# TensorE's order within a step of a graph network's edge loop: transposes, products and sums apart, a bank of the second layer behind each, relus by group

## The chip, the cores and the metric

The kernel runs on one core of a Trainium2 chip. The metric is the device time of one execution in microseconds (us). Each engine of the core (TensorE for matmuls, VectorE, ScalarE, GpSimd, SyncE) works through its own list of instructions in order and waits on semaphores that the others raise. In the profile PE is TensorE's matmuls, PEld its weight loads, DVE VectorE, ACT ScalarE, POOL GpSimd and SP SyncE. A matmul on fp32 data is two weight loads and two matmuls in the trace; a transpose, or a matmul on bf16 data, is one of each.

## What is computed

One layer of a graph network over 6,250 nodes with 128 features and 100,000 edges that are sorted by their destination, then a residual and a layer norm:

```python
msg_in = jnp.concatenate([node_features[row], node_features[col]], axis=-1)
h = jax.nn.relu(msg_in @ Wm1 + bm1)          # 256 -> 256
h = jax.nn.relu(h @ Wm2 + bm2)               # 256 -> 256
messages = h @ Wm3 + bm3                     # 256 -> 128
agg = jax.ops.segment_sum(messages, col, num_segments=num_nodes)
count = jax.ops.segment_sum(jnp.ones(...), col, num_segments=num_nodes)
agg = agg / jnp.clip(count, 1.0)[:, None]
node_in = jnp.concatenate([node_features, agg], axis=-1)
upd = jax.nn.relu(node_in @ Wn1 + bn1) @ Wn2 + bn2
return layernorm(x + node_features + upd)
```

`row` is the source of an edge and `col` its destination.

## The kernel before

The first layer is split by its input: x times the upper half of Wm1 (atab) and x times the lower half (btab, in bf16 terms) are made once for all nodes and stored in DRAM. Then 98 steps (NP) go over the edges, each with two groups of 512 edges, four tiles of 128. Wm3 is applied to the sums of a node's edges, not to each edge.

What a step p does, as its iteration of the main loop (from line 978 on) issues it:

- `fetch` (L598): for the next step, eight indirect gathers of atab rows by source on POOL (L607) and a few plain loads of btab rows on SP (L620) into one of two row buffers. Some gathers wait for a mark on TensorE's work, so that they keep its pace: `MARKS` (L588) ties gather 0 to the sums, gather 4 to the 13th matmul of a second layer, gather 6 to the first product. The loads wait for the last product that reads the buffer (`last_product`).
- `make_hot` (VectorE, L640 and L642): one-hot matrices from the destinations, to spread btab rows over edges and to sum edges into a window of nodes.
- `turned(p - 3)` (TensorE, L770): six transposes of an earlier step's sums; VectorE adds the result to the accumulator (L743, later in the loop L779).
- `node_steps(p, 0)`, and later `node_steps(p, 1)`: parts of the node network for nodes that have all their edges (TensorE L811, L817, L844), planned for certain steps.
- `first_layer(p)` (L660): for both groups 32 transposes of gathered rows (L666, 64 rows of the array each), then for both groups the products of btab rows with the one-hot matrix added on top (L674 eight of 256 columns, from step 59 on L683 sixteen of 128). All of it goes to the four banks of `ph`. Then two relus on ScalarE (L692), each over both groups, 128x1024, into h1.
- `summed(p - 2)` (L734, from step 82 on L724): eight matmuls with a one-hot matrix as weights, in columns of 32; ScalarE copies the bank out as `part` (L752).
- `second_layer` for each group of step p - 1 (L706): two banks for a group, each four matmuls (L711), and behind each bank VectorE takes the larger of it and the negative bias (L714) into `h2s`.

TensorE does all this in exactly the order written, since no scheduler moves instructions. The working banks are four tiles, used in turn by the sums, the second layer, `turned` and the node parts; whoever takes one waits until its last reader is done.

Of the kernel before, what the change touches and what calls it, by code (L numbers as in the profile page):

```python
# [13 lines left out]
AF = mybir.ActivationFunctionType  # L14
ALU = mybir.AluOpType
# [5 lines left out]
P = 128  # L21
# [9 lines left out]
def kernel(  # L31
# [511 lines left out]
    with edge, tc.tile_pool(name="wk", bufs=2) as wk, tc.tile_pool(  # L543
# [116 lines left out]
        def first_layer(got, ohts, nts, step):  # L660
            for i, ((ag, _, _), nt) in enumerate(zip(got, nts)):
                for c in range(HC):
                    for j in range(GT):
                        for h in range(nt // 2):
                            half = slice(h * HP, (h + 1) * HP)
                            nc.tensor.matmul(ph[:, i, h, c, j * HP:(j + 1) * HP], ag[half, j, c * P:(c + 1) * P],  # L666
                                             ident[half, half], is_transpose=True, start=(c == 0 and j == 0),
                                             stop=False, skip_group_check=True)
            for i, ((_, bw, paired), nt) in enumerate(zip(got, nts)):
                for c in range(HC):  # L670
                    if paired:
                        for h in range(2):
                            half = slice(h * HP, (h + 1) * HP)
                            matmul = nc.tensor.matmul(ph[:, i, h, c, :], bw[half, 0, c * P:(c + 1) * P],  # L674
                                                      ohts[half, i, :], start=False, stop=True,
                                                      skip_group_check=True)
                            pace(step + 1, "products", (i * HC + c) * 2 + h, matmul)
                            last_product[step] = matmul
                        continue
                    for k in range(2):  # L680
                        for h in range(nt // 2):
                            half = slice(h * HP, (h + 1) * HP)
                            matmul = nc.tensor.matmul(ph[:, i, h, c, k * P:(k + 1) * P],  # L683
                                                      bw[half, k, c * P:(c + 1) * P],
                                                      ohts[half, i, k * P:(k + 1) * P], start=False, stop=True,
                                                      skip_group_check=True)
                            if k == 0:
                                pace(step + 1, "products", (i * HC + c) * 2 + h, matmul)
                            last_product[step] = matmul
            h1 = next_h1()  # L690
            if nts == [GT, GT]:
                made = [nc.scalar.activation(h1[:, :, c, :].rearrange("p i (h e) -> p i h e", h=2),  # L692
                                             ph[:, :, :, c, :], AF.Relu, bias=b1[:, c:c + 1]) for c in range(HC)]
                for one in made:
                    follows(("h1", step % 2), one)
                for one in made:
                    keep(("h1", step % 2), one)
                return h1
            for i in reversed(range(len(nts))):
                nh = nts[i] // 2  # L700
                for c in range(HC):
                    nc.scalar.activation(h1[:, i, c, :nh * 2 * P].rearrange("p (h e) -> p h e", h=nh),
                                         ph[:, i, :nh, c, :], AF.Relu, bias=b1[:, c:c + 1])
            return h1

        def second_layer(h1, h2, nt, step, before):  # L706
            for j0 in range(0, nt, 2):
                ph2 = bank()
                for j in range(j0, j0 + 2):
                    for c in range(HC):  # L710
                        matmul = nc.tensor.matmul(ph2[:, j - j0, :], h1[:, c, j * P:(j + 1) * P],  # L711
                                                  w2[:, c, :], start=(c == 0), stop=(c == HC - 1))
                        pace(step + 2, "second", before + j * HC + c, matmul)
                made = nc.vector.tensor_tensor(h2[:, j0:j0 + 2, :H], ph2, nb2.to_broadcast([P, 2, H]), op=ALU.max)  # L714
                follows("copied", made)
                keep("largest", made)
# [261 lines left out]
        for i in range(NP + 7):  # L978
# [42 lines left out]
            if p == 0:  # L1021
                whole(x_part(X_FIRST, bank, (nc.scalar, nc.vector)))
# [100 lines left out]
```

## Time and profile before

| | us |
|---|---|
| median of 3 runs | 1339.16 (1331.02 to 1341.98) |
| the profiled execution | 1348.45 |
| its span | 1346.7 |
| TensorE's matmuls busy | 1237.1 |
| its weight loads busy | 935.8 |
| GpSimd busy | 793.6 |
| VectorE busy | 618.8 |
| ScalarE busy | 335.5 |

The tables take the first 85 us or so, the steps most of the rest. Matmuls overlap in the array, so the duration of one is longer than the distance to the next; distances are read from the start times of the timeline. A row of the timeline merges instructions of one kind: its start and how long it lasts in us, the engine, the line and the operation, how many, and in brackets how long the engine had been idle before it, with what ended that. A row of a window gives its length, and for each engine the busy us and the number of instructions.

### The profile page before, as it was taken

The numbers are of one execution on the slowest core, as the hardware profiler recorded it, in microseconds if no ns is written. First come the engines' busy times: TensorE is split into PE (matmuls) and PEld (weight loads), VectorE is DVE, ScalarE is ACT, GpSimd is POOL, SyncE is SP. The second block draws the span as 40 slices with busy tenths as digits, with TensorE's granted clock in tenths as the row PEclk, the third lists the DMA queues.
The fourth block names the chain that finished last, engine by engine and source line by source line (L and its number), as shares of the span: only waits on it lengthen the run. The fifth ranks groups of instructions, "written<-read, shape, count | busy, mean of one in ns | idle before, by whom it ended". The sixth has DMA issues, their size and how long they took to land.

```text
span 1346.7 us, 26320 instructions
## 1 busy us (share of the span) xinstructions
PE 1237.1 (92%) x10288; PEld 935.8 (69%) x10289; DVE 618.8 (46%) x1502; ACT 335.5 (25%) x500; POOL 793.6 (59%) x854
## 2 busy tenths in 40 slices
PE   8988998999999999999999998989988999999996
PEld 6746666776776667766766766767767677777784
DVE  6754333333333334443444443534445454555675
ACT  4741221122122112222221222221222212223232
POOL 6666665665666666666666665655655655556531
PEclk9999999999999999999999999999999899999998
DMA  7963443433433334334343444434444434344320
GB/s 224 336 207 105 124 116 99 114 106 101 112 108 112 101 107 115 106 108 129 108 110 113 123 114 118 134 111 125 131 115 120 123 111 137 107 118 122 108 58 24
DMA packets 113876, 163.66 MB, mean 122 GB/s; under 512 B 24730, under 2 KB 74592, under 8 KB 113728
## 3 DMA queue, kind: packets, MB, share of 16 engines
q0 software_dynamic: 38160, 103.75, 27.5%
q1 hardware_dynamic: 67292, 44.97, 10.8%
q10 hardware_dynamic: 8292, 13.18, 3.4%
q8 instruction: 82, 1.34, 0.4%
q14 instruction: 50, 0.41, 0.1%
HBM read 142.35 MB, written 19.86 MB: 120 GB/s over the span
## 4 chain that ended last, share of the span: by engine, by line
PE 89%; issue 6%; DVE 4%; DMA 0%; ACT 0%; POOL 0%; DVEq 0%; SPq 0%; ACTq 0%; POOLq 0%
PE bank L711 53%; PE bank L734 11%; PE ph L666 9%; PE bank L770 3%; PE ph L674 2%; PE pbt L315 2%; PE ph L683 2%; PE bank L844 2%; PE bank L811 1%; PE bank L817 1%; PE bank L724 1%; PE pxu L426 1%; DVE h L714 1%; DVE acc L779 0%; DVE span_i L267 0%
## 5 line engine op out<-in xcount | busy, mean ns | idle before, releaser
L607 POOL DMA_INDIRECT rows<-atab,srcT x784 | 746.1, 952 | 485.2 <-issue 166.8
L711 PE MATMUL bank<-w,h 128*128 128x256 f32 x3128 | 722.6, 386 | 8.0 <-DVE h L714 4.1
L711 PEld LDWEIGHTS bank<-w,h 128*128 128x128 f32 x3128 | 592.5, 192 | 139.3 <-issue 52.5
L714 DVE TENSOR_TENSOR h<-bank,nb 128x512 f32<-128x512 f32 x391 | 264.9, 690 | 600.8 <-PE bank L711 407.4
L692 ACT ACTIVATE h<-ph,b 128x1024 f32<-128x1024 f32 x194 | 205.6, 1110 | 789.2 <-remote 393.5
L666 PE MATMUL ph<-ident,rows 64*128 64x64 f32 x3128 | 134.6, 226 | 38.1 <-issue 36.6
L734 PE MATMUL bank<-h,oh 128*32 128x257 f32 x1312 | 155.5, 409 | 12.4 <-issue 1.3
L666 PEld LDWEIGHTS ph<-ident,rows 64*128 64x128 f32 x3128 | 117.2, 141 | 49.7 <-issue 46.5
L734 PEld LDWEIGHTS bank<-h,oh 128*32 128x32 f32 x1312 | 46.8, 112 | 93.8 <-issue 77.1
L743 DVE TENSOR_TENSOR acc<-acc,bank 128x96 f32 x328 | 83.5, 255 | 40.2 <-remote 18.4
L770 PEld LDWEIGHTS bank<-ident,part 64*128 64x128 f32 x681 | 31.1, 137 | 48.1 <-issue 27.6
L770 PE MATMUL bank<-ident,part 64*128 64x64 f32 x681 | 46.8, 237 | 12.6 <-DVE h L714 8.6
L315 PE MATMUL pbt<-w,xT 128*128 128x256 f32 x196 | 47.6, 388 | 5.9 <-DVE rest L340 3.0
L752 ACT COPY part<-bank 128x257 f32<-128x257 f32 x114 | 42.1, 375 | 24.4 <-PE bank L711 17.3
L315 PEld LDWEIGHTS pbt<-w,xT 128*128 128x128 f32 x196 | 36.5, 194 | 13.4 <-DVE rest L340 4.2
L674 PE MATMUL ph<-oht,rows 64*128 64x256 bf16 x472 | 40.1, 275 | 4.2 <-issue 4.2
L683 PE MATMUL ph<-oht,rows 64*128 64x128 bf16 x620 | 32.7, 225 | 10.7 <-issue 10.0
L642 DVE TENSOR_TENSOR oh<-iota_w,dloc 128x256 f32<-128x256 f32 x82 | 34.3, 418 | 0.0
L779 DVE TENSOR_TENSOR acc<-acc,bank 128x63 f32 x126 | 27.8, 221 | 13.3 <-remote 4.5
L683 PEld LDWEIGHTS <-rows 64*128 64x128 bf16 x620 | 23.2, 99 | 14.8 <-issue 14.7
L640 DVE TENSOR_SCALAR oht<-db,iota_p 128x512 bf16<-128x512 bf16 x98 | 31.8, 324 | 0.0
L674 PEld LDWEIGHTS <-rows 64*128 64x128 bf16 x472 | 24.4, 97 | 7.2 <-issue 6.3
(167 smaller groups left out, 613.0 us busy)
## 6 DMA issues: line engine op xcount, KB each, us to landing
rows<-btab SPq DMA_DIRECT2D x544, 32.0 KB
db<-reltab ACTq DMA_DIRECT2D x98, 128.0 KB
rows<-atab,srcT POOLq DMA_INDIRECT x784
btab<-acc SPq DMA_DIRECT2D x24, 384.0 KB
atab<-at SPq DMA_DIRECT2D x24, 256.0 KB
x_sb<-in_x_dram SPq DMA_DIRECT2D x5, 512.0 KB
xd<-in_x_dram SPq DMA_DIRECT2D x6, 256.0 KB
out_dram<-xd SPq DMA_DIRECT2D x6, 256.0 KB
```

The lines of the kernel that those rows point to most:

```text
L315: nc.tensor.matmul(pbt[:, a, :], xT[:, (t0 + a) * P:(t0 + a + 1) * P], w1[:, k, :], start=True, stop=True)
L607: gather = nc.gpsimd.indirect_dma_start(out=ag[:, j, :], out_offset=None, in_=atab[:, :], in_offset=bass.IndirectOffsetOnAxis(ap=idx[:, j: ...
L666: nc.tensor.matmul(ph[:, i, h, c, j * HP:(j + 1) * HP], ag[half, j, c * P:(c + 1) * P], ident[half, half], is_transpose=True, start=(c == ...
L674: matmul = nc.tensor.matmul(ph[:, i, h, c, :], bw[half, 0, c * P:(c + 1) * P], ohts[half, i, :], start=False, stop=True, skip_group_check= ...
L683: matmul = nc.tensor.matmul(ph[:, i, h, c, k * P:(k + 1) * P], bw[half, k, c * P:(c + 1) * P], ohts[half, i, k * P:(k + 1) * P], start=Fal ...
L692: made = [nc.scalar.activation(h1[:, :, c, :].rearrange("p i (h e) -> p i h e", h=2), ph[:, :, :, c, :], AF.Relu, bias=b1[:, c:c + 1]) for ...
L711: matmul = nc.tensor.matmul(ph2[:, j - j0, :], h1[:, c, j * P:(j + 1) * P], w2[:, c, :], start=(c == 0), stop=(c == HC - 1))
L714: made = nc.vector.tensor_tensor(h2[:, j0:j0 + 2, :H], ph2, nb2.to_broadcast([P, 2, H]), op=ALU.max)
L734: matmul = nc.tensor.matmul(pg[(2 * i + q) * WN:(2 * i + q + 1) * WN, :H + 1], oh[:, 2 * q + k, :], h2[:, 2 * q + k, :], start=k == 0, sto ...
L743: made = nc.vector.tensor_add(window, window, pts[q // 2][:, 0, :, k:k + WN])
L752: copied.append(nc.scalar.copy(part[:nt * WN, i], pg[:nt * WN, :H + 1]))
L770: nc.tensor.matmul(pts[r][:, i, c, :], rows, ident[half, half], is_transpose=True, start=True, stop=True, skip_group_check=True)
```

## The change

`first_layer` is cut into the transposes of a group, `first_turn(i)`, the products of a group, `first_products(i)`, and the relus of a group, `relu`. `second_layer` is cut into the matmuls of a bank, `second_bank`, and VectorE's maximum, `largest`. A step of the main loop now has TensorE do this:

turned, node part 0, transposes of group 0, bank 0 of the second layer's group 0, products of group 0, sums, bank 1 of group 0, transposes of group 1, node part 1, bank 0 of group 1, products of group 1, bank 1 of group 1.

ScalarE applies the relu to group 0 behind its products and to group 1 behind its own: four activations of 128x512 in place of two of 128x1024. The number of matmuls is the same. The core of the diff, the new loop body:

```diff
-            if p < NP:
-                s = st[p]
-                s["h1"] = first_layer(s.pop("got"), s.pop("ohts"), s["nts"], p)
+            now = st[p] if p < NP else None
+            was = st[p - 1] if 0 <= p - 1 < NP else None
+            if now:
+                first_turn(0, now["got"], now["nts"])
             if i < NP:
                 st[i]["got"] = fetch(i, [(srcT[:, 2 * i + k, :], firsts[k]) for k in range(2)], [q for q, _ in queues],
                                      paces.pop(i, {}))
-            if p == 0:
-                whole(x_part(X_FIRST, bank, (nc.scalar, nc.vector)))
+            ph2 = second_bank(was["h1"][:, 0], 0, p, 0) if was else None
+            if now:
+                first_products(0, now["got"], now["ohts"], now["nts"], p)
+                now["h1"] = next_h1()
+                relu(now["h1"], 0, now["nts"], p)
             if 0 <= p - 2 < NP:
                 pgs, matmul = summed(p - 2)
                 pace(p + 2, "sums", 0, matmul)
                 st[p - 2]["part"] = part_of(pgs, [GT] if p - 2 < PAIRED else st[p - 2]["nts"])
-            if 0 <= p - 1 < NP:
-                s = st[p - 1]
-                for j, nt in enumerate(s["nts"]):
-                    if p == NP and j == 1:
-                        load_firsts(NP - 2)
-                        load_firsts(NP - 1)
-                    second_layer(s["h1"][:, j], h2s[j], nt, p, j * GT * HC)
-                    if j == 0:
-                        node_steps(p, 1)
-            else:
-                node_steps(p, 1)
+            if was:
+                largest(ph2, h2s[0], 0)
+                largest(second_bank(was["h1"][:, 0], 2, p, 0), h2s[0], 2)
+            if now:
+                first_turn(1, now["got"], now["nts"])
+            if p == 0:
+                whole(x_part(X_FIRST, bank, (nc.scalar, nc.vector)))
+            if p == NP:
+                load_firsts(NP - 2)
+                load_firsts(NP - 1)
+            node_steps(p, 1)
+            ph2 = second_bank(was["h1"][:, 1], 0, p, GT * HC) if was else None
+            if now:
+                first_products(1, now.pop("got"), now.pop("ohts"), now["nts"], p)
+                relu(now["h1"], 1, now["nts"], p)
+            if was:
+                largest(ph2, h2s[1], 0)
+                if was["nts"][1] == GT:
+                    largest(second_bank(was["h1"][:, 1], 2, p, GT * HC), h2s[1], 2)
```

The new pieces that it calls (first_turn and first_products hold the same matmuls as before, for one group):

```diff
+        def relu(h1, i, nts, step):
+            nh = nts[i] // 2
+            made = [nc.scalar.activation(h1[:, i, c, :nh * 2 * P].rearrange("p (h e) -> p h e", h=nh),
+                                         ph[:, i, :nh, c, :], AF.Relu, bias=b1[:, c:c + 1]) for c in range(HC)]
+            for one in made:
+                follows(("h1", step % 2, i), one)
+            for one in made:
+                keep(("h1", step % 2, i), one)
+        def second_bank(h1, j0, step, before):
+            ph2 = bank()
+            for j in range(j0, j0 + 2):
+                for c in range(HC):
+                    matmul = nc.tensor.matmul(ph2[:, j - j0, :], h1[:, c, j * P:(j + 1) * P],
+                                              w2[:, c, :], start=(c == 0), stop=(c == HC - 1))
+                    pace(step + 2, "second", before + j * HC + c, matmul)
+            return ph2
+        def largest(ph2, h2, j0):
+            made = nc.vector.tensor_tensor(h2[:, j0:j0 + 2, :H], ph2, nb2.to_broadcast([P, 2, H]), op=ALU.max)
+            follows("copied", made)
+            keep("largest", made)
```

In the new kernel's lines the transposes are L675, the products L685 (and L694), the second layer L725, the sums L751 (and L741), `turned` L787, the relus L710, the maximum L731, the copy L769 and the node parts L828, L834 and L861.

Two consequences lie in the order of the calls. `fetch` of the next step now stands ahead of the products of this one, so the mark of the first product comes after the gathers have been issued: gather 6 no longer waits for it. And the last product, which the loads of btab rows wait for, now stands near the end of the step.

TensorE's order around the sums, before. A row is the line, the operation, what it writes and reads, the shape of its output, how many such follow one another, and in brackets the semaphores that it waits for; h_0 and h_1 are what VectorE's maximum left of the two groups, oh the one-hot matrices, h_859 and h_860 the two buffers h1, rows_870 and rows_871 the two row buffers.

```order
L734 MATMUL bank_856<-h_0_851,oh_865 32x257 [waits DVE_49]
L734 MATMUL bank_856<-h_0_851,oh_865 32x257
L734 MATMUL bank_856<-h_1_852,oh_865 32x257
L734 MATMUL bank_856<-h_1_852,oh_865 32x257 [waits DVE_49]
L734 MATMUL bank_856<-h_0_851,oh_865 32x257 x2
L734 MATMUL bank_856<-h_1_852,oh_865 32x257 x2
L711 MATMUL bank_857<-w_117,h_860 128x256 x4
L711 MATMUL bank_858<-w_117,h_860 128x256 [waits DVE_49]
L711 MATMUL bank_858<-w_117,h_860 128x256 x3
```

And now, at the same place of a step:

```order
L751 MATMUL bank_857<-h_0_851,oh_865 32x257 [waits DVE_49]
L751 MATMUL bank_857<-h_0_851,oh_865 32x257
L751 MATMUL bank_857<-h_1_852,oh_865 32x257 x2
L751 MATMUL bank_857<-h_0_851,oh_865 32x257 x2
L751 MATMUL bank_857<-h_1_852,oh_865 32x257 x2
L725 MATMUL bank_858<-w_117,h_860 128x256 [waits DVE_49]
L725 MATMUL bank_858<-w_117,h_860 128x256 x3
L675 MATMUL ph<-ident,rows_870 128x64 [waits DMASW7_49,Activation_49]
L675 MATMUL ph<-ident,rows_870 128x64
```

Before, four banks of the second layer in a row stood behind the sums, and the sums waited for VectorE at the first and at the fourth matmul. Now one bank stands behind them and the transposes of group 1 follow; the sums wait for VectorE once, at the first, and the first transpose of a group waits for ScalarE too.

The beginning of a step on TensorE, before, from the end of `turned` on:

```order
L770 MATMUL bank_858<-ident,part_862 128x64
L770 MATMUL bank_855<-ident,part_862 128x64
L666 MATMUL ph<-ident,rows_870 128x64 x32
L674 LDWEIGHTS rows_870
L674 MATMUL ph<-oht_863,rows_870 128x256
```

And now:

```order
L787 MATMUL bank_855<-ident,part_862 128x64
L787 MATMUL bank_856<-ident,part_862 128x64
L675 MATMUL ph<-ident,rows_870 128x64 x16
L725 MATMUL bank_857<-w_117,h_860 128x256 x4
L685 LDWEIGHTS rows_870
L685 MATMUL ph<-oht_863,rows_870 128x256
```

The 32 transposes have become 16, and a bank of the second layer stands between them and the group's products.

More of the change, by code (lines that the diff above doesn't have):

```diff
@@ L660, in first_layer @@
         def first_layer(got, ohts, nts, step):
[L661 to L668, printed above, removed]
@@ L690, in first_layer @@
-            h1 = next_h1()
[L691 to L698, printed above, removed]
+            for i in range(len(nts)):
+                first_group(i, got, ohts, nts, step)
@@ L706, in second_layer @@
         def second_layer(h1, h2, nt, step, before):
             for j0 in range(0, nt, 2):
[L708 to L714, printed above, removed]
```

63 lines of the change are left out of this document (37 added, 26 removed).

## The prediction

> **What bounds the kernel now.** I read the page's sums and its chain first, then the loop in windows, then one step engine by engine.
>
> ```profile
> PE 1237.1 (92%) x10288; PEld 935.8 (69%) x10289; DVE 618.8 (46%) x1502; ACT 335.5 (25%) x500; POOL 793.6 (59%) x854
> PE 89%; issue 6%; DVE 4%; DMA 0%; ACT 0%; POOL 0%; DVEq 0%; SPq 0%; ACTq 0%; POOLq 0%
> ```
>
> TensorE is busy 92% and holds 89% of the chain, so the loop looks like plain matmul time. The next view shows that it is not: five steps without node work, five steps with node work, and about four of the last steps.
>
> ```profile
> core 0: us, PE busy (x) PEld busy (x) DVE busy (x) ACT busy (x) POOL busy (x), PEclk, DMA share, GB/s
> 442.70:503.80 61.10, 57.80 (x474) 41.90 (x474) 21.59 (x51) 11.92 (x15) 37.90 (x41) 1.00 0.39 107
> 516.10:577.40 61.30, 60.03 (x494) 44.16 (x492) 27.55 (x62) 13.19 (x17) 38.06 (x41) 1.00 0.37 106
> 1252.80:1304.90 52.10, 51.59 (x480) 41.52 (x476) 34.43 (x97) 16.44 (x30) 26.27 (x28) 1.00 0.31 90
> ```
>
> Twenty more matmuls cost 0.2 us, though they are full-size ones; a step lasts 12.2 us either way. And at the end 480 matmuls go through in 52.10 us where 474 took 61.10. So something other than the array's time sets the length of an ordinary step. One such step:
>
> ```profile
> 479.31 2.71 PE L734 MATMUL bank<-h,oh 128*32 128x257 f32 x16
> 481.95 7.17 PE L711 MATMUL bank<-w,h 128*128 128x256 f32 x32
> 489.05 0.40 PE L770 MATMUL bank<-ident,part 64*128 64x64 f32 x6
> 489.29 0.65 PE L666 MATMUL ph<-ident,rows 64*128 64x64 f32 x14
> 490.42 0.78 PE L666 MATMUL ph<-ident,rows 64*128 64x64 f32 x18 [0.49 <-issue]
> 490.99 0.65 PE L674 MATMUL ph<-oht,rows 64*128 64x256 bf16 x8
> 491.57 0.63 PE L734 MATMUL bank<-h,oh 128*32 128x257 f32 x4
> ```
>
> From sums to sums it takes 491.57 - 479.31 = 12.26 us. Two places are long. The 16 matmuls of the sums take 481.95 - 479.31 = 2.64 us, and the transposes L666 are cut in two by a hole. Elsewhere the same pieces run clean:
>
> ```profile
> 714.03 1.08 PE L734 MATMUL bank<-h,oh 128*32 128x257 f32 x16
> 715.04 3.72 PE L711 MATMUL bank<-w,h 128*128 128x256 f32 x16
> ...
> 1258.29 1.89 PE L811 MATMUL bank<-acc,w 128*128 128x256 f32 x8
> 1260.02 3.62 PE L711 MATMUL bank<-w,h 128*128 128x256 f32 x16
> 1263.57 0.58 PE L770 MATMUL bank<-ident,part 64*128 64x64 f32 x12
> 1264.08 0.70 PE L817 MATMUL bank<-x_sb,wu 128*128 128x256 f32 x2
> 1264.71 1.21 PE L666 MATMUL ph<-ident,rows 64*128 64x64 f32 x32
> 1265.76 0.61 PE L683 MATMUL ph<-oht,rows 64*128 64x128 bf16 x16
> ```
>
> The sums take 715.04 - 714.03 = 1.01 us there, the 32 transposes 1265.76 - 1264.71 = 1.05 us. The **floor of an ordinary step** is thus 1.01 (sums) + 7.10 (L711, 481.95 to 489.05) + 0.24 (L770, to 489.29) + 1.05 (L666) + 0.58 (L674, 490.99 to 491.57) = 9.98 us. The five steps without node work average 61.10 / 5 = 12.22, which leaves 2.24 us of holes. With node work the floor is higher by 20 x 0.216 / 5 = 0.86 us (0.216 us a full matmul: 1258.29 to 1260.02, over 8), 10.84 us against 61.30 / 5 = 12.26: 1.42 us of holes. The holes stand in the dense runs of small matmuls:
>
> ```profile
> PEld bank L734 <- issue: 77.1, 178, 0.6
> PEld bank L711 <- issue: 52.5, 128, 1.8
> PEld ph L666 <- issue: 46.5, 75, 1.9
> PE ph L666 <- issue: 36.6, 69, 1.2
> ```
>
> The profile names nothing there ("issue"). The other engines of the same step tell more:
>
> ```profile
> 484.71 0.69 DVE L714 TENSOR_TENSOR h<-bank,nb 128x512 f32<-128x512 f32 x1 [3.45 <-PE bank L711]
> 487.61 0.69 DVE L714 TENSOR_TENSOR h<-bank,nb 128x512 f32<-128x512 f32 x1 [2.21 <-PE bank L711]
> 490.46 1.29 DVE L714 TENSOR_TENSOR h<-bank,nb 128x512 f32<-128x512 f32 x2 [2.16 <-PE bank L770]
> ...
> 481.58 2.12 ACT L692 ACTIVATE h<-ph,b 128x1024 f32<-128x1024 f32 x2 [9.79 <-remote]
> ...
> 1257.60 0.69 DVE L714 TENSOR_TENSOR h<-bank,nb 128x512 f32<-128x512 f32 x1 [0.32 <-PE bank L711]
> ```
>
> L711 fills its four banks at 0.216 x 8 = 1.73 us each from 481.95, so they are full near 483.7, 485.4, 487.2 and 489.05. VectorE, idle, takes them at 484.71, 487.61, 490.46 and right behind (491.1): 1.0, 2.2, 3.3 and 2.1 us late. The relus start at 481.58, some 2.2 us after the last product (479.31). In the last steps the lag is gone: L711's 16 end near 1257.40 and VectorE has the second bank at 1257.60. So in ordinary steps TensorE's news reaches the others 1 to 3 us late, and L734 needs it back: the sums read what L714 makes of the *last* bank of L711, only L770, L666 and L674 earlier. They start at 491.57, four go, and the last L714 ends at 490.46 + 1.29 = 491.75. I read an ordinary step as a **ring of late waits** (bank, L714, sums, and on), not as array time; that is why node work put into it costs nothing.
>
> **The change part by part.**
>
> *Matmuls:* none added or removed. Before, a step ran L770 6, L666 32, L674 8, L734 16, L711 32. Now a half of the transposes or of the products, or the sums, is followed by one bank of 8 full matmuls.
>
> *Array shapes:* before, a step had one run of full-size work; now it has four, so three more round trips from full to half-height work and back. From rows above: L817's two take 1264.71 - 1264.08 = 0.63 us between half-height runs where two full ones cost 0.43, so 0.20 too much; L770's twelve take 0.51 us where 12 x 0.033 = 0.40 would do, 0.11 too much. One round trip is 0.31 us, three are 0.93 us a step. Over about 97 steps that is 90 us of array time, if nothing hides it. The Trainium skill speaks against the change here: "TensorEngine Tiling (Array Packing)", section Key Properties, says that a change of tiling mode drains TensorE. It gives no figure; the 0.31 us above agrees in kind. Going by the rule without the ring, the time would rise by these 90 us, which is the third case below.
>
> *What the 0.93 us meets:* the new floor is 10.91 us without and 11.77 us with node work. Below the 12.22 and 12.26 of today that leaves 1.31 and 0.49 us a step. How many steps have node work follows from its groups:
>
> ```profile
> L811 PE MATMUL bank<-acc,w 128*128 128x256 f32 (+1 forms) x100 | 25.3, 377 | 0.3 <-DVE acc L779 0.3
> L844 PE MATMUL bank<-wu,xT 128*128 128x128 f32 (+1 forms) x98 | 20.2, 290 | 0.7 <-ACT xT L819 0.7
> L844 PE MATMUL bank<-wu,x_sb 128*128 128x128 f32 (+1 forms) x98 | 20.0, 287 | 0.5 <-ACT x_sb L819 0.4
> L817 PE MATMUL bank<-x_sb,wu 128*128 128x512 f32 (+2 forms) x36 | 14.0, 489 | 2.3 <-DVE x_sb L813 2.3
> L817 PE MATMUL bank<-rce,wu 128*128 128x512 f32 x24 | 12.3, 592 | 0.0
> ```
>
> That is 356 matmuls. The last six steps hold some 80 of them, as the timeline counts there; the other 276, at the 20 per five steps of the second window, fill 69 of the 92 steps before, three quarters. The mean room is 1.31 / 4 + 3 x 0.49 / 4 = 0.70 us. Over 92 steps the **largest gain** is 64 us, all waits gone. In the last 6 or so steps no hole is left (51.59 us busy of 52.10), so there 6 x 0.93 = 6 us are simply lost.
>
> *How much of the 64 us comes:* by the distance of the ring. Before, from the end of L711's last bank to the sums: 0.24 + 1.05 + 0.58 = 1.87 us (the fourth sum, the first that waits for that L714, some 0.4 later), against a lag of 2.1 to 3.3 us plus 0.69 for L714. Now the same path holds L787 0.24, sixteen transposes 0.53, a bank 1.73 with a round trip 0.31, four products 0.29: 3.1 us, and it is the first sum that waits now, as it takes that very bank. That covers 2.1 + 0.69 = 2.8 and falls short of 3.3 + 0.69 = 4.0. The L714s no longer come in pairs, as there is always other work between two banks. The bounds are none and all of the 64 us; I take six tenths, 38 us, being nearer to covered than not.
>
> *Relus by group:* four of 128x512 for two of 128x1024. Each costs between half and all of the present 2.12 / 2 = 1.06 us, so ScalarE gains 0 to 2.1 us a step. It is busy 11.92 / 5 = 2.4 us a step, so this hides behind TensorE, whose next use of the relus is a step later. Cover gone, it would be 2.1 us on the wait of first_turn for its half of ph; there two banks, L787, sixteen transposes, the sums and four products lie between, 2 x 1.73 + 0.24 + 0.53 + 1.01 + 0.29 = 5.5 us and a third bank behind them.
>
> *Waits:* each first_turn now also waits for the relu of the same group a step ago. It takes a separate semaphore instruction, two a step. Behind it in TensorE's order stand all sixteen transposes and the bank that follows. I take 0; if each cost as much as a whole transpose pair (0.033 us), 196 would be 6 us.
>
> *Queues:* SP's loads of b wait for the last product, now near the step's end, and serve a step later. The mark that held gather 6 back to the products is no longer set in time, so gathers 6 and 7 go sooner. POOL is busy 37.90 of 61.10 us and its rows are used a whole step later: 0.
>
> *Sum*, against the profiled execution's 1348.45 us (span 1346.7 and 1.7 around it): 1348.45 - 38 + 6 = 1316. That execution is 0.7% above the median of the runs, 1339.16, so **1307 us** on the median's scale.
>
> **The rivals.**
>
> *Supply of instructions (nearly unchanged).* TensorE's front end might need 12.2 us for a step's instructions in whatever order; holes would then only move. For it: loads of L734 come four at a time with a hole before each lot, in ordinary steps only:
>
> ```profile
> 480.59 0.17 PEld L734 LDWEIGHTS bank<-h,oh 128*32 128x32 f32 x4 [0.60 <-issue]
> 481.35 0.19 PEld L734 LDWEIGHTS bank<-h,oh 128*32 128x32 f32 x5 [0.59 <-issue]
> ```
>
> Four loads and four matmuls in 0.76 us are 95 ns an instruction; a hole of this kind also speaks of supply. Against it: 20 more matmuls cost 0.2 us, and at the end 956 instructions pass in 52.10 us (54 ns each; at that pace 188 would take 10.2 us). Then the time is as before, plus the 6 us at the end and up to 6 of the semaphores: about 1345 us. The Trainium skill, "TensorE: Matmul & The Clock Gate", section "Wait — 56ns, not 53.3ns?", knows such a bound: without hardware decoding about 62 ns per matmul. Taken for loads too, an estimate by that page is 188 x 62 ns = 11.7 us a step, which would leave things as they are; the 54 ns of the last steps do not agree with it.
>
> *The drains win (slower).* If what shortens the waits is not the distance but the lag, and the lag grows with each change of shape, the holes stay at their 2.24 and 1.42 us and the round trips come on top. From the point at which more than 0.70 of the 0.93 us a step fall on array time that no wait covers, the change loses. Place: the full banks behind first_turn and first_products. All of it is 1339 + 90 = 1429; with half of it taken by holes, 1339 + 45 = 1384. I price it at 1385. For it: the holes are partly inside a run (L734's) and not ahead of a wait. Against it: the 0.2 us for the node work, which also breaks into the step.
>
> **How the numbers follow.** Ring of waits relaxed, 0.48: 1307 us, its own range 1270 to 1330 (all 64 us give 1339 + 6 - 64 = 1281; some 10 more are left for the steps with 16 products instead of 8, which no window here counts). Supply, 0.27: 1345 us, within 1335 to 1356. Drains, 0.25: 1385 us, from 1355 to 1429. A measurement of this kernel tells about 1% from no change (the runs span 0.8%). Faster by over 1%: 0.46 of the first case, and next to nothing of the others, 0.47. Within 1%: 0.02 of the first, 0.22 of the second, 0.02 of the third, 0.26. Slower: 0.05 of the second, the rest of the third, 0.27. The range reaches from 1255 to 1388, which leaves about 0.07 below and 0.12 above.
>
> **What would show it right or wrong.** Right: the sums' 16 matmuls take near 1.0 us instead of 2.6; no hole inside the transposes; L714 starts within 1 us of its bank; a step without node work is near 11.4 us and one with it near 12, so that now node work costs something. Supply: steps still 12.2 us with and without node work, holes moved to the new places, lags as long as now. Drains: steps of 12.6 us and more, with the holes' total unchanged. The forecast is wrong if steps without node work stay above 12.1 us; if they do while the sums run clean, the wait has only changed its place.

## The result and the profile after

The change made the kernel **slower**: 1417.12 us (median of 4 runs, 1413.31 to 1421.03) against 1337.35 us, a ratio of 1.060 with a 95% interval of 1.0544 to 1.0656. The forecast was 1307 us. The profiled execution of the change has a span of 1419.3 us.

One thing has to be known before the numbers can be read: the kernel before, unchanged, took 1330 to 1353 us in three of the seven batches of runs of this study and 1148 to 1151 us in the other four, and both happened under the same chip number. One execution of 1644 us, with TensorE's granted clock at 0.65 of full speed, is left out of the long times. The first comparison and all of the prediction belong to the long times. The experiments say which they met; every ratio is against the kernel before in the same batch. "With holes" (the long times) and "without holes" (the short ones) stand for the two below; a hole is a stretch in which TensorE starts nothing and the profile names no reason.

The page of the change, its engines and its chain:

```profile
PE 1298.1 (91%) x10288; PEld 913.6 (64%) x10289; DVE 627.5 (44%) x1502; ACT 372.7 (26%) x694; POOL 796.2 (56%) x854
PE 83%; issue 7%; DVE 3%; another core or an unknown queue 2%; ACT 2%; DMA 1%; SPq 0%; POOL 0%; ACTq 0%; DVEq 0%; POOLq 0%
```

The number of matmuls is the same, TensorE is busy 61 us longer (1298.1 against 1237.1), and its share hardly moves. The windows of the same ten steps without node work and the same six with it, first of the kernel before, then of the change:

```profile
394.00:516.10 122.10, 115.44 (x944) 83.59 (x943) 44.65 (x102) 23.84 (x30) 75.56 (x80) 1.00 0.39 109
516.10:590.90 74.80, 72.28 (x594) 53.34 (x592) 33.02 (x77) 15.57 (x20) 46.25 (x50) 1.00 0.38 109
```

```profile
417.50:547.40 129.90, 118.19 (x946) 80.88 (x946) 48.23 (x110) 28.13 (x50) 76.13 (x81) 0.97 0.36 102
547.40:626.40 79.00, 74.78 (x598) 51.76 (x596) 32.69 (x76) 18.05 (x32) 45.93 (x49) 1.00 0.36 104
```

A step grew from 12.21 to 12.99 us without node work and from 12.47 to 13.17 with it: by 0.78 and 0.70 us. Over 97 steps that is 68 to 76 us, near the 73 us between the spans of the two profiled executions (1419.3 and 1346.7); the medians lie 80 us apart. One step of the change on TensorE, to be held against the step of before in the prediction:

```profile
676.00 0.66 PE L675 MATMUL ph<-ident,rows 64*128 64x64 f32 x16
676.59 1.99 PE L725 MATMUL bank<-w,h 128*128 128x256 f32 x8
678.52 0.39 PE L685 MATMUL ph<-oht,rows 64*128 64x256 bf16 x4
678.84 1.42 PE L751 MATMUL bank<-h,oh 128*32 128x257 f32 x14
681.08 0.59 PE L751 MATMUL bank<-h,oh 128*32 128x257 f32 x2 [0.82 <-issue]
681.61 1.99 PE L725 MATMUL bank<-w,h 128*128 128x256 f32 x8
683.53 0.72 PE L675 MATMUL ph<-ident,rows 64*128 64x64 f32 x16
684.18 1.99 PE L725 MATMUL bank<-w,h 128*128 128x256 f32 x8
686.10 0.39 PE L685 MATMUL ph<-oht,rows 64*128 64x256 bf16 x4
686.42 1.99 PE L725 MATMUL bank<-w,h 128*128 128x256 f32 x8
```

The transposes now run without a hole. But the sums of this step still take 681.61 - 678.84 = 2.77 us instead of 1.01. And each bank of eight full matmuls takes 1.93 us from start to start (676.59 to 678.52) where 8 x 0.216 = 1.73 would do: the price of the changes of array shape is there, four times a step (the prediction calls it drains).

Not every step looks like this one. Elsewhere in the same trace the sums run clean and the hole stands in the products:

```profile
483.20 1.08 PE L751 MATMUL bank<-h,oh 128*32 128x257 f32 x16
484.21 0.48 PE L725 MATMUL bank<-w,h 128*128 128x256 f32 x1
...
495.50 0.28 PE L685 MATMUL ph<-oht,rows 64*128 64x256 bf16 x1
497.29 0.38 PE L685 MATMUL ph<-oht,rows 64*128 64x256 bf16 x3 [1.51 <-issue]
```

These sums take 484.21 - 483.20 = 1.01 us, and the second of these products starts 1.79 us after the first. So the holes have partly moved; a table by piece stands further down.

Back to the step above, the weight loads of its sums show the form of a hole:

```profile
679.68 0.11 PEld L751 LDWEIGHTS bank<-h,oh 128*32 128x32 f32 x1 [0.27 <-issue]
680.38 0.11 PEld L751 LDWEIGHTS bank<-h,oh 128*32 128x32 f32 x1 [0.59 <-issue]
681.10 0.11 PEld L751 LDWEIGHTS bank<-h,oh 128*32 128x32 f32 x1 [0.61 <-issue]
```

One load every 0.70 us, with nothing that it waits for. The rows of VectorE and ScalarE around it:

```profile
675.88 0.69 DVE L731 TENSOR_TENSOR h<-bank,nb 128x512 f32<-128x512 f32 x1 [1.55 <-PE bank L725]
681.36 0.69 DVE L731 TENSOR_TENSOR h<-bank,nb 128x512 f32<-128x512 f32 x1 [1.31 <-PE bank L751]
...
681.25 1.27 ACT L710 ACTIVATE h<-ph,b 128x512 f32<-128x512 f32 x2 [6.03 <-PE bank L751]
```

The relu of group 0 starts at 681.25, though its products ended near 678.84: 2.4 us late, as before the change. The L731 at 681.36 says less, as it overwrites what the sums read and has to come after them in any case. The L731 at 675.88 makes the last of what the sums read. It ends at 676.57, 2.27 us before the sums start at 678.84, so this wait holds nothing up here, and the hole comes all the same.

### The profile page after: what moved, and what is told of

Its sections match the earlier page's. It is cut to its first block, busy times and chain, and to the rows that moved or that the text cites. A ratio compares the mean times of both kernels' runs of the same rounds, so it can differ in the third digit from the quotient of the medians.

```text
span 1419.3 us, 26630 instructions
## 1 busy us (share of the span) xinstructions
PE 1298.1 (91%) x10288; PEld 913.6 (64%) x10289; DVE 627.5 (44%) x1502; ACT 372.7 (26%) x694; POOL 796.2 (56%) x854
## 3 DMA queue, kind: packets, MB, share of 16 engines
q8 instruction: 83, 1.36, 0.4%
## 4 chain that ended last, share of the span: by engine, by line
PE 83%; issue 7%; DVE 3%; another core or an unknown queue 2%; ACT 2%; DMA 1%; SPq 0%; POOL 0%; ACTq 0%; DVEq 0%; POOLq 0%
PE bank L725 50%; PE bank L751 9%; PE ph L675 8%; PE ph L685 3%; PE bank L787 2%; PE pbt L315 2%; PE bank L861 2%; PE ph L694 2%; PE bank L834 2%; PE bank L828 2%; PE bank L741 1%; ACT h L710 1%; PE pxu L426 1%; DMA rows<-btab 1%
## 5 line engine op out<-in xcount | busy, mean ns | idle before, releaser
L725 PE MATMUL bank<-w,h 128*128 128x256 f32 x3128 | 793.8, 397 | 10.4 <-issue 6.8
L725 PEld LDWEIGHTS bank<-w,h 128*128 128x128 f32 x3128 | 577.0, 193 | 155.9 <-issue 61.2
L731 DVE TENSOR_TENSOR h<-bank,nb 128x512 f32<-128x512 f32 x391 | 270.3, 692 | 593.0 <-PE bank L725 294.1
L710 ACT ACTIVATE h<-ph,b 128x512 f32<-128x512 f32 x392 | 247.8, 683 | 890.8 <-PE ph L685 283.2
L751 PE MATMUL bank<-h,oh 128*32 128x257 f32 x1312 | 130.9, 401 | 37.8 <-issue 36.6
L675 PE MATMUL ph<-ident,rows 64*128 64x64 f32 x3128 | 136.5, 227 | 9.8 <-ACT h L710 6.4
L675 PEld LDWEIGHTS ph<-ident,rows 64*128 64x128 f32 x3128 | 113.8, 140 | 48.4 <-issue 31.0
L751 PEld LDWEIGHTS bank<-h,oh 128*32 128x32 f32 x1312 | 45.9, 111 | 95.1 <-issue 78.3
L685 PE MATMUL ph<-oht,rows 64*128 64x256 bf16 x472 | 52.2, 276 | 30.0 <-issue 25.7
L685 PEld LDWEIGHTS <-rows 64*128 64x128 bf16 x472 | 15.9, 94 | 76.5 <-issue 67.8
L787 PEld LDWEIGHTS bank<-ident,part 64*128 64x128 f32 x681 | 28.4, 137 | 32.5 <-issue 31.8
L769 ACT COPY part<-bank 128x257 f32<-128x257 f32 x114 | 41.4, 378 | 5.4 <-PE bank L751 2.9
L787 PE MATMUL bank<-ident,part 64*128 64x64 f32 x681 | 41.7, 235 | 0.0
L694 PEld LDWEIGHTS <-rows 64*128 64x128 bf16 x620 | 17.8, 94 | 28.7 <-issue 28.7
L694 PE MATMUL ph<-oht,rows 64*128 64x128 bf16 x620 | 31.9, 219 | 2.2 <-issue 2.2
L741 PE MATMUL bank<-h,oh 128*32 128x257 f32 x252 | 23.8, 386 | 9.8 <-issue 7.3
```

The source lines that it names most:

```text
L710: made = [nc.scalar.activation(h1[:, i, c, :nh * 2 * P].rearrange("p (h e) -> p h e", h=nh), ph[:, i, :nh, c, :], AF.Relu, bias=b1[:, c:c ...
L751: matmul = nc.tensor.matmul(pg[(2 * i + q) * WN:(2 * i + q + 1) * WN, :H + 1], oh[:, 2 * q + k, :], h2[:, 2 * q + k, :], start=k == 0, sto ...
L769: copied.append(nc.scalar.copy(part[:nt * WN, i], pg[:nt * WN, :H + 1]))
L787: nc.tensor.matmul(pts[r][:, i, c, :], rows, ident[half, half], is_transpose=True, start=True, stop=True, skip_group_check=True)
```

## The experiments

**One round trip, three round trips, full-size work, semaphore instructions, each alone in the kernel before.** Two small transposes ahead of a bank that the second layer then overwrites make a round trip of array shapes; two full matmuls at that place add array time without one.

```diff
                 ph2 = bank()
+                if before and j0 == 0:          # three round trips: if before or j0
+                    for h in range(2):
+                        nc.tensor.matmul(ph2[:, 0, h * HP:(h + 1) * HP], ident[:HP, :], ident[:HP, :HP],
+                                         is_transpose=True, start=True, stop=True, skip_group_check=True)
```

```diff
                 ph2 = bank()
+                if before and j0 == 0:
+                    for j in range(j0, j0 + 2):
+                        nc.tensor.matmul(ph2[:, j - j0, :], h1[:, 0, j * P:(j + 1) * P], w2[:, 0, :],
+                                         start=True, stop=True, skip_group_check=True)
```

```diff
+                            if c == 0 and j == 0 and h == 0 and (step, i) in loaded:
+                                tc.add_manual_dep(turn.ins, loaded[step, i].ins.name, ...)
```

> The kernel before, with two small half-height transposes of the identity put ahead of the first bank of the second layer's second group in every step; the bank is overwritten by the second layer right after, so nothing of the result changes. It adds one round trip between full-size and half-height work per step (98 in all) and moves nothing else. Drains: 0.31 us a step for the round trip and 0.06 for the two transposes, 36 us, so near 1373 us. Ring of waits with room in it: hidden like the node work, at most 8 us, near 1342. Supply of instructions (four more in the trace per step, at 54 to 95 ns): 21 to 37 us, so 1358 to 1374, not told from drains by this run alone.

> As the run with one round trip, but the two small transposes stand ahead of three of the four banks of the second layer: three round trips more per step, as in the change, with the order otherwise that of before. Drains: 3 x 0.37 x 98 = 109 us, near 1446 us; the change's own 80 us would then need no other cause. Ring of waits: the first 0.7 to 1.3 us a step are hidden, so 20 to 40 us, near 1367. Supply: 12 instructions more a step, 63 to 112 us.

> The kernel before, with two more full-size matmuls (four in the trace) ahead of the first bank of the second layer's second group in every step, written to that bank and overwritten; no change of shape. 4 x 0.216 = 0.86 us of array time a step, as in a step with node work. Ring of waits with room: hidden in steps without node work, lost in the last six and partly where node work stands already, 5 to 40 us, near 1355. If time is simply added to a step (as drains need it): 85 us, near 1422. Supply: 8 instructions more, 42 to 75 us.

> The kernel before, with the first transpose of each group also made to wait for the group's first load of b, which has landed long before. That needs a separate semaphore instruction ahead of each group's transposes, 192 more in all, as the change has them (195 more). Nothing else moves. Separate semaphore instructions as the cause: a good part of the change's 80 us, 1370 to 1420 us. Drains: nothing, within 6 us of 1337. Ring and supply: at most 192 x 0.05 = 10 us.

They met a batch without holes (before 1148.22 us). One round trip: 1191.45 (ratio 1.0362, 1.0344 to 1.0379), three: 1280.89 (1.1148, 1.112 to 1.1176), full-size work: 1228.62 (1.0687, 1.067 to 1.0705), semaphore instructions: 1150.45 (1.0012, 1.0002 to 1.0022). So a round trip costs 43 / 98 = 0.44 us and three cost 133 / 98 = 1.35, three times that; full-size work costs 80 / 98 = 0.82 of its 0.86 us. Nothing is hidden there, and the 192 semaphore instructions cost 2 us.

> One more round trip per step in the kernel before, once more, in case the chip is one on which the kernel before takes 1337 us with holes. Drains paid in full there too: 43 us as on the chip without holes. Holes that absorb a drain: under 15 us. Supply of instructions (4 more a step): 21 to 37 us.

> Three more round trips per step in the kernel before, once more. Drains paid in full: 133 us as on the chip without holes. Holes that absorb them: the part up to 2.2 us a step without and 1.4 us with node work is hidden, so under 40 us. Supply (12 more instructions): 63 to 112 us.

> Four more full-size matmuls of 0.216 us per step in the kernel before, once more. Simply added: 80 us as on the chip without holes. Holes that absorb them, as the trace of before showed for the node work: under 30 us. Supply (8 more instructions): 42 to 75 us.

> 192 separate semaphore instructions in the kernel before, once more. On a chip with holes they may cost what they did not cost without: if the holes come from a front end that each such instruction holds up, 20 to 80 us; if not, within 6 us.

The same four later met a batch with holes (before 1349.18 us): 1352.38 (1.004, 1.0011 to 1.0068), 1359.87 (1.0107, 1.0062 to 1.0153), 1353.77 (1.0036, 1.0019 to 1.0052) and 1351.54 (1.0012, 0.9994 to 1.0031). There the same work is nearly all **absorbed**: 3 us of 43, 11 of 133, 5 of 80. A constant price per instruction is out with that (12 more a step were to cost 63 us or more), and so is the notion that drains cost the same everywhere. A part of a step of the run with three round trips and holes shows where they went:

```profile
604.51 0.60 PE L674 MATMUL ph<-oht,rows 64*128 64x256 bf16 x8
605.04 1.75 PE L738 MATMUL bank<-h,oh 128*32 128x257 f32 x16
606.73 1.99 PE L715 MATMUL bank<-w,h 128*128 128x256 f32 x8
608.65 0.33 PE L711 MATMUL bank<-ident 64*128 64x64 f32 x2
608.91 1.99 PE L715 MATMUL bank<-w,h 128*128 128x256 f32 x8
```

The sums take 1.69 us (605.04 to 606.73) instead of 2.64: the holes shrink as the banks' stretch grows. Averaged over 45 steps (from the sixth on), a step takes 12.34 us before and 12.34, 12.41 and 12.41 us with one round trip, three round trips and full-size work. Without holes the same steps take 10.21, 10.64, 11.56 and 11.04 us.

**The change itself, and its parts taken back.**

> The change as it is, beside the kernel before on a chip of its own, since the first runs of experiments found the kernel before at 1148 us and without holes there. Drains at the price of those runs (43 us for 98 round trips with two small transposes each, less 0.06 us a step for these: 0.38 us a round trip; by the trace of before 0.31): 3 x 97 trips, 90 to 112 us above before, so 1238 to 1260 where before takes 1148. If the change's cost were the holes of TensorE's front end instead, it would cost next to nothing where there are no holes, at most 20 us.

Without holes: 1241.88 us against 1149.15 (1.0816, 1.0788 to 1.0843). The change costs 93 us there. It made no holes and removed none, as there were none; its windows of the same ten and six steps:

```profile
359.40:467.60 108.20, 108.20 (x942) 77.31 (x940) 45.77 (x103) 27.97 (x50) 76.65 (x81) 1.00 0.43 123
467.60:537.80 70.20, 70.20 (x598) 50.48 (x598) 33.37 (x77) 18.04 (x32) 45.76 (x49) 1.00 0.41 117
```

TensorE is busy all of the time, 10.82 and 11.70 us a step.

> The change with the relus of both groups behind the last products, as halves still but not by group; TensorE's order stays. Drains: as the change itself, within 6 us. Relus by group as a part of the cost (or of a gain): more than 10 us away from the change.

```diff
-                now["h1"] = next_h1()
-                relu(now["h1"], 0, now["nts"], p)
...
-                relu(now["h1"], 1, now["nts"], p)
+                now["h1"] = relus(now["nts"], p)
```

1283.49 us, 42 above the change itself. So giving group 0 its relus early is worth 42 us in the new order. Where the time goes:

```profile
609.50 0.40 PE L787 MATMUL bank<-ident,part 64*128 64x64 f32 x6
610.17 0.71 PE L675 MATMUL ph<-ident,rows 64*128 64x64 f32 x16 [0.27 <-ACT h L710]
```

The next step's transposes want ph back and stand behind the late relus: L787 to L675 takes 0.67 us where the change needs 0.23.

> The kernel before with its relus in four halves by group (128x512) in place of two of 128x1024, all behind the last product; TensorE's order is untouched. Drains: within 6 us of before, since ScalarE's longer work hides. If the halves themselves cost time on the path, up to 2.1 us a step by the prediction's bound.

```diff
-                made = [nc.scalar.activation(h1[:, :, c, :]..., ph[:, :, :, c, :], ...) for c in range(HC)]
+                for i in range(2):
+                    made = [nc.scalar.activation(h1[:, i, c, :]..., ph[:, i, :, c, :], ...) for c in range(HC)]
```

With holes, 1337.10 us against 1337.97 (0.9999, 0.9973 to 1.0024): in the old order halves alone do nothing there. Without holes they were not run, so what they cost where nothing is absorbed stays open.

> The change with two runs of full-size work a step in place of four: the transposes of both groups together, one bank of the second layer, the products of both groups and the sums, then the other three banks; relus by group. One round trip more than before instead of three. Drains: a third of the change's cost, 30 to 38 us above before. Standing the sums and products apart as such (waits, relus, semaphores) as the cause: nearly the change's whole cost.

A miss: 1327.43 us against 1149.15 (1.1559, 1.1531 to 1.1588), worse than the change. The relu of group 0 stood between the two groups' products, and the products of group 1 waited for it:

```profile
606.10 0.39 PE L685 MATMUL ph<-oht,rows 64*128 64x256 bf16 x4
607.85 0.39 PE L685 MATMUL ph<-oht,rows 64*128 64x256 bf16 x4 [1.36 <-ACT h L710]
608.17 1.08 PE L751 MATMUL bank<-h,oh 128*32 128x257 f32 x16
```

1.75 us from four products to the next, every step: 1.43 us more than the 0.32 that four take, 140 us in all. The next run puts the relus behind both.

> The run with two runs of full-size work once more, but with the relus of group 0 issued behind the products of both groups, so that the products of group 1 don't stand behind ScalarE (each step waited 1.36 us there). Drains: one round trip more than before, 0.31 us by the trace of before, 30 us; near 1179 where before takes 1148. If something else of the order cost time, it would stay above 1200.

```diff
                 first_products(0, now["got"], now["ohts"], now["nts"], p)
+                first_products(1, now.pop("got"), now.pop("ohts"), now["nts"], p)
                 now["h1"] = next_h1()
                 relu(now["h1"], 0, now["nts"], p)
+                relu(now["h1"], 1, now["nts"], p)
```

> The change with three runs of full-size work: the transposes of group 1 moved from ahead of the second node part to ahead of their own products, so that two banks of the second layer meet. Two round trips more than before. Drains: two thirds of the change's 93 us, 62 us, near 1210. If the cost isn't by round trip, it lies near the change's 1242 or near 1179.

```diff
-            if now:
-                first_turn(1, now["got"], now["nts"])
...
             if now:
+                first_turn(1, now["got"], now["nts"])
                 first_products(1, now.pop("got"), now.pop("ohts"), now["nts"], p)
```

Without holes (before 1149.51 us): 1174.76 (1.022, 1.0203 to 1.0238) and 1211.22 (1.0529, 1.0512 to 1.0547). One, two and three round trips more cost 25, 62 and 93 us: 0.26, 0.32 and 0.32 us each over 97 steps. That is the change's whole cost without holes, built up one round trip after another.

> Two runs of full-size work a step, no separate semaphore instructions, once more, in case the chip is one with holes. There three added round trips in the kernel before cost 11 us and full-size work 5. Drains alone: hidden, under 10 us. The order itself, where the sums and products stand behind a single bank instead of behind dense work, as the cause of new holes: a good part of the change's 80 us, 25 to 80.

> Three runs of full-size work a step, once more, in case the chip is one with holes. Drains alone: hidden but for 5 to 15 us. The order itself: between the run with two and the change, 40 to 80 us. On a chip without holes: 25 and 62 us again.

Both came out without holes again (1174.30 and 1210.92 us against 1149.64), so they repeat the two above and leave their question open.

**The first node part moved.**

> The kernel before with the first node part of a step moved from between the transposes of turned and those of the gathered rows to just ahead of the second layer, so that full-size work meets full-size work. It takes one round trip out of each step that has matmuls in that node part, a third to a half of 98. Drains: 10 to 19 us less than before. Drains that other work hides: within 5 us of before. A later node part that makes others wait: slower than before.

```diff
-            node_steps(p, 0)
             if p in X_LATER:
...
+            node_steps(p, 0)
             if 0 <= p - 1 < NP:
```

Without holes, 1148.36 us against 1149.15 (0.9993, 0.9983 to 1.0003): nothing. The expectation had counted wrongly. In ordinary steps the node matmuls already stand between two banks; only about six of the last steps have some between transposes, as L817 in the rows of the prediction.

**The kernel before without holes.**

> The kernel before unchanged, for its profile on a chip where it takes 1148 us. Drains: no holes, steps of 9.98 us without and 10.84 us with node work, as worked out from the clean pieces. Ring of waits: VectorE still late behind the banks, the same holes. If the lag is TensorE's own news held up by a starved front end, it is gone together with the holes.

1148.52 us. The steps of its TensorE, and VectorE and ScalarE beside them:

```profile
610.90 1.08 PE L734 MATMUL bank<-h,oh 128*32 128x257 f32 x16
611.91 7.17 PE L711 MATMUL bank<-w,h 128*128 128x256 f32 x32
619.02 0.39 PE L770 MATMUL bank<-ident,part 64*128 64x64 f32 x6
619.25 1.16 PE L666 MATMUL ph<-ident,rows 64*128 64x64 f32 x32
620.25 0.60 PE L674 MATMUL ph<-oht,rows 64*128 64x256 bf16 x8
620.78 1.08 PE L734 MATMUL bank<-h,oh 128*32 128x257 f32 x16
...
615.67 0.69 DVE L714 TENSOR_TENSOR h<-bank,nb 128x512 f32<-128x512 f32 x1 [1.03 <-PE bank L711]
617.40 0.69 DVE L714 TENSOR_TENSOR h<-bank,nb 128x512 f32<-128x512 f32 x1 [0.74 <-PE bank L711]
619.13 0.69 DVE L714 TENSOR_TENSOR h<-bank,nb 128x512 f32<-128x512 f32 x1 [1.03 <-PE bank L711]
...
611.02 2.12 ACT L692 ACTIVATE h<-ph,b 128x1024 f32<-128x1024 f32 x2 [8.38 <-PE ph L674]
```

The step lasts 620.78 - 610.90 = 9.88 us. The banks are full near 613.6, 615.4, 617.1 and 618.8; VectorE takes the last three at 615.67, 617.40 and 619.13, 0.3 us behind. The relus follow the products (610.90) by 0.12 us. The holes and the lag are gone together, in the same program.

## Why the prediction was wrong

*What bounds the kernel.* That an ordinary step is longer than its array work was right, and so was the **floor**: 9.98 and 10.84 us were worked out from clean pieces, 9.87 and 10.73 are what the run without holes shows (98.70 us for ten steps, 64.40 for six):

```profile
334.00:432.70 98.70, 98.70 (x946) 79.41 (x948) 46.06 (x104) 23.84 (x30) 74.62 (x80) 1.00 0.48 132
432.70:497.10 64.40, 64.40 (x594) 51.68 (x592) 33.07 (x74) 15.56 (x20) 48.85 (x52) 1.00 0.48 133
```

*Array shapes.* Right: three round trips were put at 0.93 us a step and 90 us. Without holes a step grows by 10.82 - 9.87 = 0.95 and 11.70 - 10.73 = 0.97 us, and the change costs 93 us. In the table below all of the 0.95 lies in the pieces that the change cuts up: second layer 0.59, transposes 0.25, products 0.11; the sums and `turned` are as before. The new floors of 10.91 and 11.77 were 10.82 and 11.70. The rule that the prediction cited from the Trainium skill, "TensorEngine Tiling (Array Packing)", section Key Properties, that a change of tiling mode drains TensorE, agrees with this: 0.26 to 0.32 us for each round trip of the change.

*What the 0.93 us meets.* Right in kind for work added inside the stretch of banks, as the runs with holes show (11 of 133 us remain), but not for the change.

*How much of the gain comes.* **This step failed.** It read the holes as a ring of waits (bank, L714, sums) that a longer distance would relax. The late L714 was taken for a cause. Two observations speak for an effect. The change did lengthen the way: in the step shown L731 ended 2.27 us before the sums began, and 1.76 us were lost inside the sums even so. And without holes the distance of before, 1.87 us, is enough, since the last L714 ends at 619.82 and the sums start at 620.78, with 0.96 us in hand. What is late with holes seems to be TensorE's own supply of instructions (its front end): loads come one by one every 0.70 us with no wait named, and the others hear of finished work only when they are through. That the one makes the other late is read from the rows and was not tried apart. A longer way between bank and sums did nothing for it. By step, the holes were 12.21 - 9.87 = 2.34 and 12.47 - 10.73 = 1.74 us before, and 12.99 - 10.82 = 2.17 and 13.17 - 11.70 = 1.47 after: they shrank by 0.17 and 0.27 us, while 0.95 came on top. The six tenths, 38 us over 92 steps or 0.41 us a step, needed them to shrink by 0.93 + 0.41 = 1.34.

Where the holes went shows in the same four windows of ten steps without node work, each piece counted from its first start to the start of the next piece:

| us a step | before, without holes | before, with holes | change, without holes | change, with holes |
|---|---|---|---|---|
| sums | 1.01 | 2.55 | 1.00 | 1.88 |
| second layer | 7.11 | 7.11 | 7.70 | 8.32 |
| transposes of rows | 0.99 | 1.65 | 1.24 | 1.24 |
| products | 0.53 | 0.61 | 0.64 | 1.25 |
| `turned` | 0.23 | 0.30 | 0.23 | 0.30 |
| step | 9.87 | 12.21 | 10.82 | 12.99 |

The change took the hole out of the transposes and 0.66 us out of that in the sums; new ones of 0.62 and 0.61 us stand in the second layer and the products. The wait was not relaxed: the lost time changed its place.

*Relus by group.* The range was right (0.683 us each in the page of the change, against 0.53 to 1.06). That they hide behind TensorE was nearly right: its transposes waited for L710 6.4 us in all in the change with holes and 2.8 us without. The 42 us without the early relus concern another order, in which both groups' relus stand behind the last products.

*Waits and queues.* The separate semaphore instructions cost 2 us, at most 4 by the intervals (ratio 1.0012 in both conditions). The queues of SP and POOL show no wait that explains a difference: TensorE's products waited for the loads of b three times, 3.1 us in all. Neither these loads nor gather 6, now without its mark, were tried apart.

*The rivals.* "The drains win" was the case that came, and its sign of recognition, the holes' total nearly unchanged, is what the windows show; its full price of 1429 was nearer than the 1385 given. Its reason was only half of it: the lag does not grow with changes of shape, as three round trips elsewhere cost 11 us under the same conditions. "Supply" was nearer the truth about the holes than the ring, and its sign, holes moved to new places, came as well; but it isn't a fixed cost per instruction.

*What stays open.* First, why the same program has these holes in some batches and not in others. The commonest instructions of the engines last as long in both (medians: L711 379 ns, L714 692, the gathers 949 and 947), and the granted clock is 1.00 in both pairs of windows of the kernel before. So what differs seems to be TensorE's front end alone; what feeds it more slowly was not found. Second, why with holes the same three round trips are absorbed between banks and not in the new order. One observation may bear on it. The separate semaphore instructions can be seen in the trace as they pass through TensorE's front end. Without holes, in the kernel before with such instructions, the one of group 0 passes 16 or 17 matmuls ahead of its transposes; with holes, 3 to 10 ahead (600 to 680 us of the span in both). There the front end never has its full lead, so all time won between the banks is of use to it. In the change with holes, the instruction of group 0 passes 16 matmuls ahead, exactly as in the change without holes: at that place it has its full lead and can use no more time, and right after come the dense pieces, in which it falls behind again (the instruction of group 1 passes 5 to 13 ahead where it is 20 without holes). That would lose the time of the drains each step. It is argued from these positions and not shown; the two runs meant for it met no holes.

## What to carry to other kernels

Count the changes of array shape in an order written by hand: full-size work put between half-height and column work cost about 0.3 us for every round trip here, and they add up. A neighbour that starts late is not yet a cause: ask first whether the bounding engine's own news is late, for instance by work that should have fitted between. And a floor made of clean pieces of one's own trace was good to 1% here; where a kernel stands far above it with no wait named, find out in a second run, on another occasion, whether the gap belongs to the kernel at all before tuning against it.

## What the runs showed of the hardware that was not expected

- The same program took 1148 to 1151 us in some batches and 1330 to 1353 in others, with the same durations of single instructions and a granted clock of 0.99 and 0.98; the difference is holes in TensorE's stream that no semaphore in the profile explains.
- With such holes, work added between full-size banks is nearly free (11 us for 133); without them it counts in full or nearly so (0.82 of 0.86 us a step). An experiment on one of the two says little of the other.
- In the holes, weight loads come at distances of 0.70 us, and VectorE and ScalarE learn of finished matmuls 1 to 3 us late; without holes 0.1 to 0.3 us.
- A round trip of array shapes costs 0.26 to 0.32 us with work as in the change and 0.44 us with two tiny transposes, these included.
- Products of one group waited 1.36 us for the activation that reads the other group's banks of the same PSUM tile, when it was issued between them. The trace has a semaphore of ScalarE on that product, so this wait lies in the program.
